# Two-layer graph kernel in fp32: quarter-block weight loads, turns of the scores moved inside the weight stage, half of layer 1's statistics on ScalarE, and another order in the ends

## The chip, the cores and the metric

The kernel runs on one core of one Trainium2 chip. The metric is the device time of that core in microseconds (us), as the median of several executions. One further execution was taken by the hardware profiler; the rows quoted below come from it.

## The reference

The input x has 64 graphs of 256 nodes with 512 features. Both layers normalise, rectify, mix over the graph and add to x. Cut to what matters:

```python
h = relu(layernorm(x))                               # layer 0
q, k, v = h @ Wq.T, h @ Wk.T, h @ Wv.T
rel = adj.T * (q @ k.T)
x = x + (rel / norm(rel, axis=2)) @ v
h = relu(layernorm(x))                               # layer 1
x = x + (adj @ h) @ weight + bias
```

All matrices are fp32. The kernel folds Wq and Wk into one matrix M, so that the scores are g h with g = M h, and it multiplies by two-by-two block schemes of seven products (Strassen and Winograd), some with a second level inside.

## The kernel before

**Tiling.** Two graphs make a pair, so there are 32 pairs (NP = 32); a pair has four chunks of 128 nodes. A ring of five buffers (`x_ring`) holds x for five pairs. The work of several pairs is interleaved: while pair i is in layer 1, pair i+1 is in its scores, pair i+2 in its projections g and v, and pair i+3 is being normalised and transposed.

**Stages.** `before_pairs` forms M from Wq and Wk, looks whether the low bits of adj are zero (this selects between two versions of the loop; with these inputs the exact one runs), transposes adj and Wv, and normalises pair 0. `first_pairs` fills the pipeline, `steady(i)` runs for i = 1 to 28, `last_pairs` drains it. In `steady(i)` the order is: `attend_and_v` (attention of pair i, rest of v), `scores` of pair i+1, `g_and_v` of pair i+2, the gather `py` with adj (`gather_steps`), and the weight stage `mix_and_v` (layer 1's weight product, with the remaining g and v products between).

**What sets the order.** TensorE, VectorE and ScalarE run in exactly the order in which the code emits, written out by hand. A stage is a list of products, and a dictionary `{slot: steps}` says which steps of other engines are emitted behind which product. Each engine works its own list from the front; a step that has to wait holds everything behind it on that engine. A product is followed by its `take`: ScalarE copies the PSUM bank where it is the first into its place, VectorE adds it otherwise.

**Banks.** In `winograd_steps` and `two_levels` most products accumulate into one bank, `bank_a`: product 1, then 6, 7 and 4 on top of it. Each is read by its `take` before the next may be added. The products are called a1, c5, a6, a7, a4; g1 to g4 are the small second-level products in `bank_e` and `bank_d`.

**The names that the change touches.** `norm` (L322) gives the steps of a normalisation: per chunk BN_STATS and BN_AGGREGATE (L333, L334) on VectorE, `root` (L337, L338), `end` (L341, L342) and the ReLUs on ScalarE (L345). `ln1` is layer 1's normalisation; its first four steps are called `halves` in `steady`. `turns` are four VectorE transposes (L592, `turned<-placed`) of the scores, which an earlier step `place` has moved by 16 DMAs (L589) from `rel` to `placed`; `rel_steps` (L176 to L179) form the operands of the attention out of `turned`. `second_of_y` gives `y_second`, eight small VectorE operations for the second level of the weight product. `take` of the weight product is L776, the second level's is L537, that of the scores is L562, that of the attention L672.

In `steady`, `turns` come behind the last product of the gather:

```python
run_steps(y_products, {0: v_steps[1:2], 2: y_steps[0:1], 3: turns})
```

**DMA queues.** At the start SyncE's queue (SP) carries Wq in four row blocks and x of pair 0, ScalarE's queue (ACT) carries adj, then Wk in four row blocks; Wv and the next x follow on ScalarE's queue from inside the M product. Before each pair's transposes 16 small DMAs (L443) move h from one layout to another on SP.

Of the kernel before, what the change touches and what calls it, by code (L numbers as in the profile page):

```python
# [19 lines left out]
def kernel(  # L20
# [61 lines left out]
    X, H, HL, G, V, R, H2, Y, HL2, Y2, second_h = ({} for _ in range(11))  # L82
# [13 lines left out]
    adj_sb = work.tile([P, NC, N], F32, tag="placed", name="adj_sb")  # L96
    w_sb = const.tile([P, DC, D], F32, name="w_sb")
    bias_bc = const.tile([P, D], F32, name="bias_bc")
    nc.scalar.dma_start(out=adj_sb, in_=adj.rearrange("(c p) n -> p c n", p=P))
    for e in range(DC):  # L100
        nc.sync.dma_start(out=wq_sb[:, e], in_=wq[e * P : (e + 1) * P, :])
        nc.scalar.dma_start(out=wk_sb[:, e], in_=wk[e * P : (e + 1) * P, :])
    load(0)
    ones = const.tile([P, 1], F32, name="ones")
    nc.gpsimd.memset(ones, 1.0)
    warm = work.tile([P, P], F32, tag="turned", name="warm")
    nc.gpsimd.memset(warm, 0.0)
    ident = const.tile([P, P], F32, name="ident")
    make_identity(nc, ident)

    def load_wv():
        nc.scalar.dma_start(out=wv_sb, in_=wv.rearrange("(c p) d -> p c d", p=P))

    def load_w_and_bias():
        nc.scalar.dma_start(out=w_sb, in_=weight.rearrange("(c p) d -> p c d", p=P))
# [4 lines left out]
    def flat(t):  # L120
        return t.rearrange("p b c d -> p (b c) d")
# [158 lines left out]
    def run_steps(steps, side):  # L280
        for at, step in enumerate(steps):
            step()
            run(side.get(at, ()))
# [35 lines left out]
        return product  # L319


    def norm(src):  # L322

        st = small.tile([P, TC, 6], F32, tag="st", name="st")
        mv = small.tile([P, TC, 2], F32, tag="mv", name="mv")
        rs = small.tile([P, TC], F32, tag="rs", name="rs")
        nb = small.tile([P, TC], F32, tag="nb", name="nb")  # L330

        def chunk(c):
            nc.vector.bn_stats(st[:, c, :], src[:, c, :])  # L333
            nc.vector.bn_aggr(mv[:, c, :], st[:, c, :])  # L334

        def root():
            nc.vector.tensor_scalar(rs, mv[:, :, 1], 0.0, EPS, op0=ALU.max, op1=ALU.add)  # L337
            nc.scalar.activation(rs, rs, AF.Sqrt)  # L338

        def end():  # L340
            nc.vector.reciprocal(rs, rs)  # L341
            nc.vector.scalar_tensor_tensor(nb, mv[:, :, 0], -1.0, rs, op0=ALU.mult, op1=ALU.mult)  # L342

        def relu(dst, c):
            nc.scalar.activation(  # L345
                dst, src[:, c, :], AF.Relu, bias=nb[:, c : c + 1], scale=rs[:, c : c + 1]
            )

        return [(lambda c=c: chunk(c)) for c in range(TC)], root, end, relu

    def norm_by_scalar(src):

# [37 lines left out]
    def ln0(i):  # L390

        if i == 0:
            H[i] = blocks.rearrange("p c d e -> p c (d e)")
        else:
            H[i] = work.tile([P, TC, D], F32, tag="hy", name=f"h_{i}")
        h = H[i]
        chunks, root, end, relu = norm(flat(X[i]))
        return chunks, root, end, [(lambda c=c: relu(h[:, c, :], c)) for c in range(TC)]

    def relus_of_h(i, relu):  # L400
# [287 lines left out]
        ], side)  # L688


    def ln1(i, exact):


        xt = flat(X[i])
        chunks, root, end, relu = norm(xt)
# [61 lines left out]

    def second_of_y(i, pool_tag="h2"):

        room = work.tile([P, 2, 3, P], F32, tag=pool_tag, name=f"ys2_{i}")  # L760
# [62 lines left out]
    def before_pairs():  # L823
# [16 lines left out]
        stats, root, end, relus = ln0(0)  # L840

        def look():
            nc.vector.tensor_single_scalar(
                low, adj_sb.rearrange("p c n -> p (c n)").bitcast(I32), 0xFFF, op=ALU.bitwise_and
            )
            nc.vector.tensor_reduce(low_max, low, axis=mybir.AxisListType.X, op=ALU.max)
            pf = ps_m.tile([P, 512], F32, tag="pm", name="pf")
# [22 lines left out]
        def take(t, k, bank, first):  # L870
# [4 lines left out]
            else:  # L875
                nc.vector.tensor_add(dst, src, dst)

        look()
        transpose_adj()
        run([right_steps[1], left_steps[1]])  # L880
        winograd(product_weights_moving(m_left, m_factors), take, {
            0: [load_wv, left_steps[2], right_steps[2]],
            1: [left_steps[3], left_steps[0]],
            2: [right_steps[0]] + stats[0:1] + [lambda: load(1, nc.scalar)],
            3: stats[1:4] + [root, lambda: load(2, nc.scalar)],
            4: [end] + relus + [right_steps[3]],
            5: m_steps[0:3] + [transpose_wv],
            6: m_steps[3:4],
        }, early=True)
# [47 lines left out]
    def first_pairs(exact):  # L937
# [50 lines left out]
        if exact:  # L988
            nc.vector.tensor_copy(adjt_r, adjt_sb)
        g, v = g_and_v(2, by_slot(layer_1(parts), {  # L990
            1: h_second + [inverse], 2: turned3[0:4], 3: scales + [place],
            4: add_bias(0) + turned3[4:6], 5: turned3[6:8], 6: sums3[0:1],
        }))
        v_steps, rel_steps = attend_operands(1)
# [6 lines left out]
        run(y_steps[1:2])  # L1001
        mixed = mix_and_v(0, g, v, {
            0: y_steps[2:4] + totals[0:2], 1: y_second[0:4] + totals[2:4],
            2: y_second[4:8] + [mean] + row_squares[0:2], 3: v_steps[1:2] + row_squares[2:4],
            4: turns + rel_steps[0:2] + norm0[0:2], 5: rel_steps[2:4] + v_steps[2:3],
        })
        return norm0[2], v_steps[3:4], mixed, v

    def steady(i, exact, relu0, v_last, mixed, v):
# [3 lines left out]

        gs = g_operands(i + 1)
        relus0 = relus_of_h(i + 3, relu0)
        stats, root, end, relus, uppers, lowers = ln1(i, exact)
        halves = [stats[b * NC + t] for t in range(NC) for b in range(NB)]
        attend_and_v(i, mixed, v, {
            0: relus0[0:2] + v_last, 1: relus0[2:4] + gs[0:1], 2: gs[1:2],
            3: gs[2:3], 4: gs[3:4] + halves[0:1], 5: halves[1:2],  # L1020
        })
        place_blocks(i + 3)
        if i + 4 < NP:
# [1 line left out]
        HL2.pop(i + 1)  # L1025
        h_second = second_h.pop(i + 2)()
        masks, squares, norm_root, inverse, scales, place, turns = scores(i + 1, {
            0: halves[2:3], 1: halves[3:4] + h_second[0:1], 2: [root] + h_second[1:4],
            3: [end] + relus[0:1], 4: relus[1:2],
        }, inside=True)  # L1030
        turned, sums = transpose_blocks(i + 3)
# [7 lines left out]
            5: lowers[3:4] + sums[1:3], 6: sums[3:4] + v_steps[0:1],  # L1039
        })  # L1040
        y_products, y_steps = gather_steps(i, exact)
        run_steps(y_products, {0: v_steps[1:2], 2: y_steps[0:1], 3: turns})
        y_second = second_of_y(i)
        totals, row_squares, mean, root0, end0, relu0 = [], [], [], [], [], None
        if i + 4 < NP:
# [3 lines left out]
        mixed = mix_and_v(i, g, v, {  # L1049
            0: y_steps[2:4] + totals[0:2], 1: y_second[0:4] + totals[2:4],  # L1050
            2: y_second[4:8] + mean + row_squares[0:2],
            3: rel_steps[0:2] + row_squares[2:4], 4: root0 + rel_steps[2:4] + end0,
            5: v_steps[2:3],
        })
        return relu0, v_steps[3:4], mixed, v
# [1 line left out]
    def last_pairs(exact, relu0, v_last, mixed, v):  # L1057
# [59 lines left out]
            m["a1"], m["c5"], m["a6"], m["g1"], lambda: run([m["a7"], m["c"]]), m["g2"], m["a4"],  # L1117
            m["g3"],
        ], {
            0: y_second[0:4] + [root], 1: y_second[4:8] + [end] + relus[0:2] + uppers[0:2],  # L1120
            4: lowers[0:2] + relus[2:4], 5: uppers[2:4] + add_bias(c), 7: lowers[2:4],
        })
        y_products, y_steps = gather_steps(c, exact)
# [44 lines left out]
```

## Time and profile before

| | |
|---|---|
| median of 3 executions | 1706.22 us (1706.12 to 1707.53) |
| the profiled execution's own time | 1703.48 us |
| its span in the profile | 1701.4 us |
| TensorE (PE) busy | 1684.2 us, 99% |
| VectorE (DVE) busy | 1472.9 us, 87% |
| ScalarE (ACT) busy | 811.3 us, 48% |
| GpSimd (POOL) busy | 226.7 us, 13% |
| period of an undisturbed steady pair (gather at 524.85 to gather at 576.57) | 51.72 us |

The profiled execution's own time is 2.1 us above its span (what lies around the span) and 2.7 us below the median. A row of the timeline gives start, duration, engine, source line, operation, output and inputs, and in brackets how long the engine was idle before it and what released it. A matmul's end is modelled, so consecutive rows overlap: eight records of 128x256 are drawn 1.89 us long, but the next group starts 1.73 us later.

### The profile page before, as it was taken

What the parts mean: (1) busy time and instruction counts of PE and PEld (TensorE: products, weight loads), DVE (VectorE), ACT (ScalarE), POOL (GpSimd) and SP (SyncE); (2) the same over time, 40 slices, a digit from 0 to 9 for tenths busy, and PEclk for the clock granted to TensorE, in tenths of its full rate; (3) what the DMA queues carried; (4) which work ended last, traced back from release to release, by engine and by line L of the source; (5) the groups of instructions that cost most, each with busy time, mean ns of one, the idle gap of its engine ahead of it and who ended that gap; (6) DMA issues with size and microseconds to landing.
All of it is one profiled execution on the core that took longest, in us unless ns stands there. A gap on an engine that the chain in (4) does not pass through costs nothing.

```text
span 1701.4 us, 28459 instructions
## 1 busy us (share of the span) xinstructions
PE 1684.2 (99%) x10274; PEld 1530.6 (90%) x10274; DVE 1472.9 (87%) x3312; ACT 811.3 (48%) x1835; POOL 226.7 (13%) x191
## 2 busy tenths in 40 slices
PE   9999999999999999999999999999999999999997
PEld 7979999999899999999999999999999999999986
DVE  7788889888898888898888988888988889888677
ACT  4455444545445554445544455454455544453331
POOL 1211100111101111001111001110011110011111
PEclk9999999999999999999999999999999999999999
DMA  7414332234332233332343322443323433223101
GB/s 247 63 26 87 84 78 57 55 77 87 79 62 68 53 87 85 77 60 63 65 87 80 83 50 50 87 87 77 60 67 60 87 83 80 55 47 62 38 25 53
DMA packets 425734, 122.56 MB, mean 72 GB/s; under 512 B 398064, under 2 KB 398832, under 8 KB 425584
## 3 DMA queue, kind: packets, MB, share of 16 engines
q1 hardware_dynamic: 412992, 80.28, 25.6%
q0 software_dynamic: 8432, 32.51, 5.2%
q10 hardware_dynamic: 4160, 7.87, 1.3%
q8 instruction: 83, 1.36, 0.3%
q14 instruction: 67, 0.55, 0.1%
HBM read 38.27 MB, written 33.55 MB: 42 GB/s over the span
## 4 chain that ended last, share of the span: by engine, by line
PE 91%; DVE 4%; SPq 2%; DMA 1%; ACT 1%; issue 1%; DVEq 0%; ACTq 0%
PE bank_a L302 24%; PE bank_a L290 12%; PE bank_a L314 7%; PE bank_c L302 6%; PE bank_e L528 6%; PE bank_a L665 6%; PE py L742 6%; PE bank_d L528 5%; PE bank_c L314 3%; PE bank_c L290 3%; PE bank_c L665 3%; PE bank_e L481 3%; SPq L589 2%; PE bank_d L481 2%; PE bank_b L314 2%; PE bank_b L665 1%
## 5 line engine op out<-in xcount | busy, mean ns | idle before, releaser
L726 POOL TENSOR_TENSOR x_ring<-x_ring,bias_bc 128x512 f32<-128x512 f32 x128 | 187.2, 1483 | 667.3 <-DVE rel L562 406.2
L302 PE MATMUL bank_a<-wv_t,ht 128*128 128x256 f32 x768 | 181.7, 379 | 0.0
L290 PE MATMUL bank_a<-ht,m_t 128*128 128x256 f32 x768 | 181.4, 379 | 0.0
L290 PEld LDWEIGHTS bank_a<-ht,m_t 128*128 128x128 f32 x768 | 145.9, 190 | 19.8
L302 PEld LDWEIGHTS bank_a<-wv_t,ht 128*128 128x128 f32 x768 | 143.5, 190 | 18.3
L714 DVE TENSOR_TENSOR h<-h2c,h 128x512 fp32r<-128x512 f32 x128 | 85.4, 689 | 80.0 <-ACT h L710 80.0
L516 ACT COPY v<-bank_a 128x512 f32<-128x512 f32 x96 | 55.1, 574 | 206.5 <-PE bank_a L302 206.5
L367 ACT ACTIVATE blocks<-x_ring,sm 128x512 f32<-128x512 f32 x112 | 80.8, 722 | 125.3 <-DVE sm L364 123.5
L742 PE MATMUL py<-adjt_r,h 128*128 128x256 f32 x1024 | 127.1, 281 | 0.5 <-DVE h L714 0.4
L345 ACT ACTIVATE h2c<-x_ring,nb,rs 128x512 f32<-128x512 f32 x128 | 97.3, 809 | 58.0 <-DVE nb L342 51.9
L302 PE MATMUL bank_a<-w_t,ys 128*128 128x256 f32 x512 | 121.4, 380 | 2.2 <-DVE x_ring L776 2.2
L742 PEld LDWEIGHTS py<-adjt_r,h 128*128 128x128 f32 x1024 | 120.9, 189 | 1.0 <-DVE h L714 0.9
L797 POOL DMA_DIRECT2D out_dram<-x_ring x31 | 24.0, 773 | 723.3 <-issue 522.9
L380 ACT ACTIVATE h<-x_ring,nb,rs 128x512 f32<-128x512 f32 x112 | 82.0, 802 | 66.0 <-PE bank_e L528 66.0
L302 PEld LDWEIGHTS bank_a<-w_t,ys 128*128 128x128 f32 x512 | 96.7, 190 | 16.4 <-DVE x_ring L776 3.0
L746 ACT COPY yt<-py 128x512 f32<-128x512 f32 x128 | 74.9, 588 | 70.4 <-PE py L742 47.3
L776 DVE TENSOR_TENSOR x_ring<-bank_a,x_ring 128x512 f32<-128x512 f32 x128 | 87.9, 687 | 23.2 <-PE bank_a L302 23.2
L314 PE MATMUL bank_a<-ht,gt 128*128 128x128 f32 x744 | 101.2, 279 | 0.0
L333 DVE BATCH_NORM_STATS2 st<-x_ring 128x6 f32<-128x512 f32 x144 | 97.6, 678 | 0.4
L560 ACT COPY rel<-bank_a 128x256 f32<-128x256 f32 x96 | 35.7, 372 | 129.6 <-PE bank_a L314 111.1
L314 PEld LDWEIGHTS bank_a<-ht,gt 128*128 128x128 f32 x744 | 90.4, 192 | 2.8
L453 DVE STREAM_TRANSPOSE ht<-blocks 128x256 f32<-128x256 f32 x248 | 87.7, 407 | 0.7 <-DMA blocks<-h 0.7
(223 smaller groups left out, 4012.5 us busy)
## 6 DMA issues: line engine op xcount, KB each, us to landing
blocks<-h SPq DMA_DIRECT2D x496, 64.0 KB, 2.3
out_dram<-x_ring POOLq DMA_DIRECT2D x31, 1024.0 KB, 4.8
x_ring<-in_x_dram SPq DMA_DIRECT2D x28, 1024.0 KB, 5.6
placed<-rel SPq DMA_DIRECT2D x496, 32.0 KB, 2.0
x_ring<-in_x_dram ACTq DMA_DIRECT2D x4, 1024.0 KB, 5.3
wq_sb<-in_L_gnn_Wq_dram SPq DMA_DIRECT2D x4, 256.0 KB, 4.8
wk_sb<-in_L_gnn_Wk_dram ACTq DMA_DIRECT2D x4, 256.0 KB, 6.0
wv_sb<-in_L_gnn_Wv_dram ACTq DMA_DIRECT2D x1, 1024.0 KB, 5.6
```

The costliest lines, as they stand in the source:

```text
L290: nc.tensor.matmul(bank[:, e * HT_ : (e + 1) * HT_], right[n][:, d, ts(e, P)], left[n][:, d, :], start=(start and e == 0 and d == 0), stop ...
L302: nc.tensor.matmul(bank[:, b * HD : (b + 1) * HD], left[n][:, d, ts(b, P)], right[n][:, d, :], start=(start and b == 0 and d == 0), stop=( ...
L314: nc.tensor.matmul(bank[:, ts(b, P)], right[n][:, d, ts(b, P)], left[n][:, d, ts(b, P)], start=(start and b == 0 and d == 0), stop=(d == H ...
L333: nc.vector.bn_stats(st[:, c, :], src[:, c, :])
L345: nc.scalar.activation(dst, src[:, c, :], AF.Relu, bias=nb[:, c : c + 1], scale=rs[:, c : c + 1])
L453: nc.vector.transpose(ht[:, d, half].rearrange("p (b n) -> p b n", b=NB), by_half[:, :, half, d])
L528: nc.tensor.matmul(out, left[k][n], right[k][n], start=start, stop=True, skip_group_check=True)
L665: nc.tensor.matmul(bank[:, ts(b, HD)], left[n][:, b], right[n][:, b], start=(start and b == 0), stop=True, skip_group_check=True,)
L714: nc.vector.tensor_sub(dst[:, 1, c, :], whole_h[c], dst[:, 0, c, :].bitcast(F32))
L726: (lambda c=c: add(xt[:, c, :], xt[:, c, :], bias_bc, ALU.add)) for c in range(TC)
L742: nc.tensor.matmul(pm[:, d, :], left[:, b * NC + m, ts(d0 + d, P)], right, start=(n == 0), stop=(n == len(terms) - 1),)
L776: nc.vector.tensor_add(xt[block], bank.rearrange("p (b e) -> p b e", b=NB), xt[block])
```

## The change

1. Wq and Wk are loaded by quarter blocks (two row chunks by half the columns) in the order in which M's seven products use them; adj comes behind Wk, x of pair 0 behind Wq, and Wv directly behind adj, all before the M product.
2. In `before_pairs` the look at adj, its verdict (`find`) and the transpose of adj move from ahead of the M product to the products numbered 3 and 4 in it; pair 0's statistics become those of item 3.
3. `norm` takes a scratch tile `junk`. With it, chunks 0 and 2 get their sums and their squared deviations from ScalarE (four activations with an accumulator), and two small VectorE operations (`minus`, `variances`) connect them; chunks 1 and 3 stay on VectorE. It is used for pair 0's first normalisation and for layer 1 in `steady`. The scratch lies in the tile of `second_of_y`, made larger.
4. In `steady` the `turns` move from behind the gather into the weight stage, to slot 3, ahead of `rel_steps[0:2]`.
5. In `first_pairs` the scaling and placing of pair 1's scores move from slot 3 to slot 1 of `g_and_v`, ahead of `h_second`, and `turns` from slot 4 to slot 3 of `mix_and_v`.
6. In `last_pairs` the eight operations `y_second` are spread: four behind c5 and four behind a6, in the last two weight stages.

```diff
+    for k in range(2):
+        for j in range(2):
+            block = (slice(None), slice(j * HC, (j + 1) * HC), slice(k * HD, (k + 1) * HD))
+            nc.sync.dma_start(out=wq_sb[block], in_=wq.rearrange("(c p) d -> p c d", p=P)[block])
+            nc.scalar.dma_start(out=wk_sb[block], in_=wk.rearrange("(c p) d -> p c d", p=P)[block])
     nc.scalar.dma_start(out=adj_sb, in_=adj.rearrange("(c p) n -> p c n", p=P))
-    for e in range(DC):
-        nc.sync.dma_start(out=wq_sb[:, e], in_=wq[e * P : (e + 1) * P, :])
-        nc.scalar.dma_start(out=wk_sb[:, e], in_=wk[e * P : (e + 1) * P, :])
     load(0)
+    nc.scalar.dma_start(out=wv_sb, in_=wv.rearrange("(c p) d -> p c d", p=P))
...
+        def totals():
+            for c in (0, 2):
+                nc.scalar.activation(
+                    junk, src[:, c, :], AF.Copy, scale=1.0 / D, accum_out=mv[:, c, 0:1]
+                )
+        def squares():
+            minus = small.tile([P, TC], F32, tag="minus", name="minus")
+            nc.vector.tensor_single_scalar(minus[:, 0::2], mv[:, 0::2, 0], -1.0, op=ALU.mult)
+            for c in (0, 2):
+                nc.scalar.activation(
+                    junk, src[:, c, :], AF.Square, bias=minus[:, c : c + 1],
+                    accum_out=mv[:, c, 1:2],
+                )
+        def variances():
+            nc.vector.tensor_scalar(
+                mv[:, 0::2, 1], mv[:, 0::2, 1], 0.0, 1.0 / D, op0=ALU.max, op1=ALU.mult
+            )
...
+        if junk is not None:
+            chunks = [totals, squares, variances] + chunks[1::2]
...
-        look()
-        transpose_adj()
         run([right_steps[1], left_steps[1]])
         winograd(product_weights_moving(m_left, m_factors), take, {
-            0: [load_wv, left_steps[2], right_steps[2]],
+            0: [left_steps[2], right_steps[2]],
             1: [left_steps[3], left_steps[0]],
-            2: [right_steps[0]] + stats[0:1] + [lambda: load(1, nc.scalar)],
-            3: stats[1:4] + [root, lambda: load(2, nc.scalar)],
-            4: [end] + relus + [right_steps[3]],
+            2: [right_steps[0], lambda: load(1, nc.scalar)],
+            3: stats[0:1] + [look] + stats[1:2] + [right_steps[3], lambda: load(2, nc.scalar)],
+            4: stats[2:] + [root, end] + relus + [find, transpose_adj],
             5: m_steps[0:3] + [transpose_wv],
...
 # first_pairs
-            1: h_second + [inverse], 2: turned3[0:4], 3: scales + [place],
+            1: [inverse] + scales + [place] + h_second, 2: turned3[0:4],
...
-            2: y_second[4:8] + [mean] + row_squares[0:2], 3: v_steps[1:2] + row_squares[2:4],
-            4: turns + rel_steps[0:2] + norm0[0:2], 5: rel_steps[2:4] + v_steps[2:3],
+            2: y_second[4:8] + [mean] + row_squares[0:2],
+            3: turns + v_steps[1:2] + row_squares[2:4], 4: rel_steps[0:2] + norm0[0:2],
+            5: rel_steps[2:4] + v_steps[2:3],
...
 # steady
-            3: gs[2:3], 4: gs[3:4] + halves[0:1], 5: halves[1:2],
+            3: gs[2:3], 4: stats[0:1] + gs[3:4], 5: stats[1:2],
...
-            0: halves[2:3], 1: halves[3:4] + h_second[0:1], 2: [root] + h_second[1:4],
+            0: stats[2:4], 1: stats[4:5] + h_second[0:1], 2: [root] + h_second[1:4],
...
-        run_steps(y_products, {0: v_steps[1:2], 2: y_steps[0:1], 3: turns})
+        run_steps(y_products, {0: v_steps[1:2], 2: y_steps[0:1]})
...
-            3: rel_steps[0:2] + row_squares[2:4], 4: root0 + rel_steps[2:4] + end0,
+            3: turns + rel_steps[0:2] + row_squares[2:4], 4: root0 + rel_steps[2:4] + end0,
...
 # last_pairs
-            0: y_second[0:4] + [root], 1: y_second[4:8] + [end] + relus[0:2] + uppers[0:2],
+            0: [root], 1: y_second[0:4] + [end] + relus[0:2] + uppers[0:2], 2: y_second[4:8],
...
-        ], {0: y_steps[2:4], 1: y_second})
+        ], {0: y_steps[2:4], 1: y_second[0:4], 2: y_second[4:8]})
```

More of the change, by code (lines that the diff above doesn't have):

```diff
@@ L80 @@
     ps_m = ctx.enter_context(tc.tile_pool(name="ps_m", bufs=8, space=bass.MemoryType.PSUM))
-    X, H, HL, G, V, R, H2, Y, HL2, Y2, second_h = ({} for _ in range(11))
+    X, H, HL, G, V, R, H2, Y, HL2, Y2, second_h, junk = ({} for _ in range(12))
     ring = [const.tile([P, NB, NC, D], F32, name=f"x_ring{n}") for n in range(5)]
@@ L109 @@
     make_identity(nc, ident)
-    def load_wv():
-        nc.scalar.dma_start(out=wv_sb, in_=wv.rearrange("(c p) d -> p c d", p=P))
     def load_w_and_bias():
@@ L319, in product_of_tokens, with norm @@
         return product
-    def norm(src):
+    def norm(src, junk=None):
         st = small.tile([P, TC, 6], F32, tag="st", name="st")
@@ L347, in relu @@
             )
-        return [(lambda c=c: chunk(c)) for c in range(TC)], root, end, relu
+        chunks = [(lambda c=c: chunk(c)) for c in range(TC)]
+        if junk is not None:
+            chunks = [totals, squares, variances] + chunks[1::2]
+        return chunks, root, end, relu
     def norm_by_scalar(src):
@@ L396, in ln0 @@
         h = H[i]
-        chunks, root, end, relu = norm(flat(X[i]))
+        chunks, root, end, relu = norm(flat(X[i]), None if i else h[:, 0, :])
         return chunks, root, end, [(lambda c=c: relu(h[:, c, :], c)) for c in range(TC)]
@@ L688, in attend_and_v, with ln1 @@
         ], side)
-    def ln1(i, exact):
+    def ln1(i, exact, junk=None):
         xt = flat(X[i])
-        chunks, root, end, relu = norm(xt)
+        chunks, root, end, relu = norm(xt, junk)
         H2[i] = work.tile([P, 2, TC, D], F32R if exact else F32, tag="h2", name=f"h2_{i}")
@@ L758, in second_of_y @@
     def second_of_y(i, pool_tag="h2"):
-        room = work.tile([P, 2, 3, P], F32, tag=pool_tag, name=f"ys2_{i}")
+        rooms = 6 if pool_tag == "hs2" else 10
+        room = work.tile([P, rooms * P], F32, tag=pool_tag, name=f"ys2_{i}")
+        junk[i] = room[:, 6 * P :]
+        room = room[:, : 6 * P].rearrange("p (k r n) -> p k r n", k=2, n=P)
         factors, steps = {}, []
@@ L846, in look, with find @@
             nc.vector.tensor_reduce(low_max, low, axis=mybir.AxisListType.X, op=ALU.max)
+        def find():
             pf = ps_m.tile([P, 512], F32, tag="pm", name="pf")
@@ L1015, in steady @@
         relus0 = relus_of_h(i + 3, relu0)
-        stats, root, end, relus, uppers, lowers = ln1(i, exact)
-        halves = [stats[b * NC + t] for t in range(NC) for b in range(NB)]
+        stats, root, end, relus, uppers, lowers = ln1(i, exact, junk.pop(i - 1))
         attend_and_v(i, mixed, v, {
             0: relus0[0:2] + v_last, 1: relus0[2:4] + gs[0:1], 2: gs[1:2],
-            3: gs[2:3], 4: gs[3:4] + halves[0:1], 5: halves[1:2],
+            3: gs[2:3], 4: stats[0:1] + gs[3:4], 5: stats[1:2],
         })
```

## The prediction

> **What bounds the kernel now.** I read the page's busy table first, then the waits of TensorE, then the timeline of one steady pair, of pair 0 and of both ends.
>
> ```profile
> PE 1684.2 (99%) x10274; PEld 1530.6 (90%) x10274; DVE 1472.9 (87%) x3312; ACT 811.3 (48%) x1835; POOL 226.7 (13%) x191
> ```
>
> The waits of TensorE (us in total, times, longest):
>
> ```profile
> PE bank_c L302 <- DVE yt L177: 2.3, 5, 0.6
> PE bank_a L302 <- DVE x_ring L776: 2.2, 3, 1.1
> PE bank_e L528 <- DVE x_ring L537: 1.8, 2, 1.6
> ```
>
> TensorE is the bound: 17 us idle in 1701. A wait given to TensorE is added to the span; work taken from VectorE or ScalarE helps only where TensorE waits. The five waits on L177 are those where `turns` sat waiting for their DMAs, the 1.6 is in pair 0, those on L776 in the last weight stages. So the change aims at real idle time, but a small one. The question is what its moves put in the way.
>
> The weight stage of one steady pair (start us, duration us):
>
> ```profile
> 588.42 0.41 DVE L537 TENSOR_TENSOR x_ring<-bank_d,x_ring 128x256 f32<-128x256 f32 x1
> 588.75 0.41 DVE L176 TENSOR_TENSOR rel<-turned 128x256 f32<-128x256 f32 x1
> ...
> 589.20 0.43 DVE L177 TENSOR_TENSOR turned<-turned 128x256 f32<-128x256 f32 x1
> ...
> 589.96 0.69 DVE L776 TENSOR_TENSOR x_ring<-bank_a,x_ring 128x512 f32<-128x512 f32 x1 [0.33 <-PE bank_a L302]
> ...
> 590.65 0.61 PE L481 MATMUL bank_e<-ht,m_t 128*128 128x128 f32 x4
> 591.09 1.89 PE L302 MATMUL bank_a<-w_t,yt 128*128 128x256 f32 x8
> ```
>
> L776 takes product a7 out of `bank_a`; a4 (591.09) is added to that bank next. VectorE waits 0.33 us for a7, ends the take at 590.65, and a4 starts 0.44 later. That is all the cover here: from 582.05 to 589.63 VectorE ran without a gap.
>
> Pair 0 already has its `turns` in the weight stage, a slot later:
>
> ```profile
> 123.30 1.41 DVE L592 STREAM_TRANSPOSE turned<-placed 128x256 f32<-128x256 f32 x4
> ...
> 126.87 0.41 DVE L537 TENSOR_TENSOR x_ring<-bank_e,x_ring 128x256 f32<-128x256 f32 x1
> ...
> 127.43 0.46 PE L528 MATMUL bank_e<-w_t,yt 128*128 128x128 f32 x2 [1.63 <-DVE x_ring L537]
> ```
>
> There TensorE loses 1.63 us: the take behind the transposes is late. This is the change's placing, seen in the kernel before.
>
> [...] rows keep the order of the code, and groups drawn 1.89 us long follow each other after 1.73; I use starts. [...] Wk's last block, issued at 4.7 beside x of pair 0, came into use at 10.6.
>
> **The change part by part.**
>
> *Turns in the weight stage (28 steady pairs).* Removed: four transposes behind the gather, where VectorE had cover; its take of a1 waited 0.32 us for TensorE after them. There c5 started 0.10 late (1.83 after a1 against 1.73). That comes back in every pair, and in the five pairs whose DMAs were late another 0.45: -2.2 us together. Added at 588.75, ahead of L176: the transposes, whose start-to-start is 1.34 (579.75 to 581.09). With everything 0.08 earlier, they run from 588.67; L176 depends on the last one and follows at 590.1, L177 at 590.55, the take of a7 at 590.95, done at 591.65 with its 0.05 of signal. TensorE, 0.10 earlier, was ready for a4 at 590.99: it waits about 0.67, **+0.57 a pair** against before. What follows keeps its distance: VectorE stays 0.4 behind a4 as before (take 593.38, bank ready 593.02), so nothing is won back. By the bounds: 0.45 if the dependent steps cost nothing extra, 0.70 if they cost 0.1 each. Queued behind the transposes are the takes of a7, g2 and g4, the root of the next normalisation (ScalarE) and its DMAs on SP; all slip with TensorE, none is waited for.
>
> *Half the statistics of layer 1 (28 pairs).* Removed from VectorE: two BN_STATS and BN_AGGREGATE, 0.8 each; added: two operations of 0.17. That relief lies in the attention and scores stages, where in these rows TensorE waits for VectorE once:
>
> ```profile
> 611.41 1.06 PE L314 MATMUL bank_b<-ht,g 128*128 128x128 f32 x8
> ...
> 611.90 0.42 DVE L562 TENSOR_TENSOR rel<-bank_a,rel 128x256 f32<-128x256 f32 x1
> ...
> 612.37 1.16 PE L314 MATMUL bank_a<-ht,gt 128*128 128x128 f32 x8
> ```
>
> The last product follows the take of `rel` by 0.05. VectorE had run to it without a gap from 608.04, the third BN_STATS: 3.86 us. After: ScalarE copies v at 603.92 to 604.50, totals two chunks at 0.82 each (L361's rows) to 606.14; `minus` at 606.32 (behind L537, as the first statistics were); two squares at 0.84 (L367's rows) from 606.52 to 608.18; `variances` at 608.2; the remaining chunks' BN_STATS only at 608.3. From there the same 3.86 to the take: 612.15, **+0.25 a pair**. Bounds: 0 (accumulator reads overlap) to 0.40. ScalarE's first copy of `rel` slips from 608.03 to 608.2 and ends at 608.57, before the 608.73 at which a6 needs the bank: no cost, with 0.15 us of cover.
>
> *Start.* The first matmul of M stood at 6.47, the next waited for Wk until 7.99, then to 10.58; from 11.98 to 26.0 TensorE had no gap. With quarter blocks and adj behind them the first products run from 4.9 (end of the warm-up). In the trace packets of 1,024 bytes took 46 ns and those of 2,048 bytes 84, so the 2.1 MB in short rows take 128 x 46 ns = 5.9 us on each of 16 DMA engines: all landed near 8.5, c5 at 9.2 against 11.98. With pf and the transposes of adj (0.6) inside, TensorE is through M about 2.1 us earlier. But what then releases it is pair 0's normalisation:
>
> ```profile
> 19.07 2.93 ACT L345 ACTIVATE blocks<-x_ring,nb,rs 128x512 f32<-128x512 f32 x4 [0.68 <-DVE nb L342]
> ...
> 22.36 1.91 PE L431 MATMUL pt<-ident,blocks 128*128 128x128 f32 x16
> ...
> 23.32 2.05 ACT L434 COPY ht<-pt 128x512 f32<-128x512 f32 x4
> ```
>
> x of pair 0 landed at 12.1; now it comes behind all of Wq and shares with adj and Wv: 8.2 + 2.1 MB at 0.385 MB per us = 13.7 (totals can't start before the copy of a6, 13.4, anyway). Then totals 1.64, `minus` 0.25, squares 1.69, `variances` 0.1, two chunks 1.5, to the ReLU 0.85: first ReLU at 19.8; ReLUs 2.83, then on ScalarE adj's copy 0.5 (before at 6.67), Wv's 0.94, M's 0.48: the first `ht` copy at 24.55, against 23.32. **+1.2**, from -1.5 (if the chain is as short as before) to +2.5. SP's and GpSimd's reading of the branch value slips from 6.3 to 20; their next work stood at 36 and 23.5. ScalarE's table load waits behind Wv's issue, to 7.4; its first copy is needed at 10.9.
>
> *Pair 0.* Earlier `turns` run about 119.8 to 121.1; the take of a7 then delays a4 by 0.3 and g4 by 0.3 instead of 1.63, and smaller gaps behind it (0.34 together) mostly stay: -1.2. But the scales (1.71, L582) now stand on ScalarE ahead of the copy of g's a6 (99.06): it slips to 100.7, and a7 (100.36) waits until 101.35: +1.0. **-0.2**, from -1.5 to +1.
>
> *Ends.* In the last two weight stages four small operations (1.06) leave the way to the take of a6: the waits of 0.78 and 1.14 before a7 shrink, by 0.94 (with the `end` before it) and 1.05. The other four, now behind a6, end 0.8 us before g2 needs them. **-2.0**, from -2.5 to -1.
>
> *Sum:* 28 x 0.82 = 23.0, -2.2, +1.2, -0.2, -2.0: **+19.8 us** on the profiled execution (span 1701.4, own time 1703.5, so 1723.3). The median is 2.7 above that execution; on it, 1726.0.
>
> **Rivals.** *The transposes fit (faster).* If VectorE's lateness at L776 stays inside 0.33 idle + 0.44 of cover, so if they cost it under 0.77 instead of 1.34, a4 isn't held, c5 keeps its 0.10 in 28 pairs (-2.8), and without the scores' wait: -2.8 - 2.2 + 1.2 - 0.2 - 2.0 = -6.0, 1700 us. For it: five late pairs exist, and VectorE does less in all. Against it: L592's own rows, and pair 0's 1.63. *Nothing to tell.* The added wait is some 0.2 a pair and eats the gains: within 3 us of 1706. Needs both terms at a third. *ScalarE late as well (slower still).* If the squares end 0.15 us later than worked out, a6 of the scores waits too; 0.3 a pair gives +8 more, 1734. For it: it is a chain of six handovers, each estimated at 0.03 to 0.05. That the moves aren't made is excluded by the order of the instructions: the four transposes stand between L537 and L176 in every steady pair.
>
> **How the numbers follow.** Slower by the forecast's mechanism, ScalarE's included: 0.83; the transposes fit: 0.13; nothing to tell: 0.04. A measurement of this kernel can tell about 0.2%, 3.4 us, from no change. The likeliest gives 1726. The lows of the two steady terms, 28 x 0.45, and the other terms at their lows give 1711; the highs, 28 x 1.1 less 2.2 with the start at +2.5, give 1735. Range 1713 to 1736, leaving out the faster case.
>
> **What would show it.** In the changed profile: a steady period near 52.5 instead of 51.72; in TensorE's waits `bank_a` on x_ring's take (L804 there) some 0.6 us in 28 pairs, and no waits on `yt`; the last scores product later by 0.25 behind its take; the first `ht` copy after 24; no wait above 0.3 before a7 in the last two stages. It would be wrong if the steady period is at or below 51.7, or if a4 follows g4 without a gap.

## The result, and the profile after

The changed kernel takes 1731.51 us (median of 4 executions, 1731.14 to 1732.0), the kernel before 1706.88 us beside it: ratio 1.0144, 95% interval 1.0126 to 1.0162, so slower by 24.6 us. The forecast was 1726.0 in a range of 1713 to 1736, and slower with 0.83. The profiled execution of the changed kernel took 1732.0 us, its span is 1730.1 at a granted clock of 0.999. The span of before was 1701.4, so the two traces differ by 28.7, about 4 more than the medians: the profiled execution of before lay 3.4 below the median it has here, that of after 0.5 above.

The busy table and the chain that ended last, of the changed kernel:

```profile
PE 1692.6 (98%) x10274; PEld 1533.0 (89%) x10274; DVE 1430.8 (83%) x3254; ACT 895.2 (52%) x2067; POOL 220.3 (13%) x191
...
PE 60%; DVE 25%; SPq 5%; ACT 4%; issue 3%; DMA 2%; DVEq 0%; ACTq 0%
```

VectorE has 42 us less to do than before and ScalarE 84 more, yet the chain now runs through VectorE for 25% of the span (4% before, where TensorE had 91%). Less busy is not earlier. The waits of TensorE (us in total, times, longest):

```profile
PE bank_a L302 <- DVE x_ring L804: 18.5, 29, 0.7
PE bank_a L314 <- DVE rel L587: 2.2, 13, 0.3
PE bank_e L553 <- DVE x_ring L562: 1.6, 2, 1.4
```

L804 is the take of the weight product (L776 before): 3 waits have become 29, one for each of 28 steady pairs and one in the ends. The waits on `yt`, where the transposes behind the gather had waited for their DMAs, are gone.

One steady weight stage of the changed kernel (start us, duration us, idle before it in brackets):

```profile
598.82 1.41 DVE L617 STREAM_TRANSPOSE turned<-placed 128x256 f32<-128x256 f32 x4
600.27 0.43 DVE L176 TENSOR_TENSOR rel<-turned 128x256 f32<-128x256 f32 x1
600.54 0.61 PE L506 MATMUL bank_e<-ht,m_t 128*128 128x128 f32 x4
...
601.07 0.68 DVE L804 TENSOR_TENSOR x_ring<-bank_a,x_ring 128x512 f32<-128x512 f32 x1
601.81 1.99 PE L302 MATMUL bank_a<-w_t,yt 128*128 128x256 f32 x8 [0.66 <-DVE x_ring L804]
```

The four transposes, L176, L177 and the take follow each other without a gap, and a4 (601.81) starts 0.06 behind the end of the take. It follows the small product before it (600.54, g4 in the prediction) by 1.27 us, against 0.44 before: it is 0.83 late, of which the row draws 0.66 as idle, because consecutive rows overlap by 0.17. And the scores of the same pair:

```profile
619.02 0.17 DVE L354 TENSOR_SCALAR mv<-mv 128x2 f32<-128x2 f32 x1 [0.49 <-ACT ys L348]
...
622.22 1.06 PE L314 MATMUL bank_b<-ht,g 128*128 128x128 f32 x8
622.96 0.41 DVE L587 TENSOR_TENSOR rel<-bank_a,rel 128x256 f32<-128x256 f32 x1
623.43 1.16 PE L314 MATMUL bank_a<-ht,gt 128*128 128x128 f32 x8
```

VectorE stands 0.49 us for ScalarE's squares (L348) in front of `variances`, and everything behind it is late: the last scores product follows `bank_b`'s group by 1.21 instead of 0.96.

Where the 28.7 us lie, from the starts of the gathers `py` (pair number as in the code):

| stretch | before | after | difference | forecast |
|---|---|---|---|---|
| start to gather of pair 0 | 107.24 | 110.60 | +3.36 | +1.2 (start), +1.0 (scales) |
| to gather of pair 1 | 54.06 | 53.22 | -0.84 | -1.2 |
| 27 steady periods | 27 x 51.836 | 27 x 52.787 | +25.70 | +20.8, with the next row |
| one more period | 51.72 | 52.39 | +0.67 | |
| from gather of pair 29 to the end | 88.82 | 88.63 | -0.19 | -2.0 |
| sum | 1701.4 | 1730.1 | +28.7 | +19.8 |

The first steady pair's scores lie in the second row, ahead of the gather of pair 1. With the statistics alone (stats_only, below) that row is 54.32, so 0.26 of it is their wait, and the earlier `turns` of pair 0 gave 1.10.

### The profile page after: what moved, and what is told of

It is laid out like the page before. It is cut to its first block, busy times and chain, and to the rows that moved or that the text cites. A ratio compares the mean times of both kernels' runs of the same rounds, so it can differ in the third digit from the quotient of the medians.

```text
span 1730.1 us, 28627 instructions
## 1 busy us (share of the span) xinstructions
PE 1692.6 (98%) x10274; PEld 1533.0 (89%) x10274; DVE 1430.8 (83%) x3254; ACT 895.2 (52%) x2067; POOL 220.3 (13%) x191
## 3 DMA queue, kind: packets, MB, share of 16 engines
q8 instruction: 83, 1.36, 0.3%
## 4 chain that ended last, share of the span: by engine, by line
PE 60%; DVE 25%; SPq 5%; ACT 4%; issue 3%; DMA 2%; DVEq 0%; ACTq 0%
PE bank_a L302 15%; PE bank_a L290 13%; PE py L767 7%; DVE x_ring L804 6%; SPq L468 5%; PE bank_c L302 4%; PE bank_a L690 3%; PE bank_c L290 3%; PE bank_a L314 3%; PE bank_e L553 3%; DVE turned L617 2%; PE bank_e L506 2%; PE bank_d L506 2%; DVE st L335 2%; DVE ys L178 2%
## 5 line engine op out<-in xcount | busy, mean ns | idle before, releaser
L751 POOL TENSOR_TENSOR x_ring<-x_ring,bias_bc 128x512 f32<-128x512 f32 x128 | 180.7, 1432 | 686.2 <-ACT h2c L367 656.0
L697 DVE TENSOR_TENSOR x_ring<-bank_a,x_ring 128x512 f32<-128x512 f32 x116 | 79.5, 685 | 39.6 <-PE bank_a L690 39.6
L804 DVE TENSOR_TENSOR x_ring<-bank_a,x_ring 128x512 f32<-128x512 f32 x128 | 87.6, 685 | 17.6 <-PE bank_a L302 17.5
L492 ACT COPY g<-bank_a 128x512 f32<-128x512 f32 x96 | 56.0, 583 | 56.6 <-PE bank_a L290 56.6
```

What stands on the lines that cost most here:

```text
L751: (lambda c=c: add(xt[:, c, :], xt[:, c, :], bias_bc, ALU.add)) for c in range(TC)
L804: nc.vector.tensor_add(xt[block], bank.rearrange("p (b e) -> p b e", b=NB), xt[block])
```

## The experiments

### How many transposes fit into the weight stage

Theory: the loss comes only from VectorE being late at the take of a7, and there is a limit below which this costs nothing. Rival: ScalarE's statistics carry the loss, or each transpose costs in proportion. Three kernels from the changed one, with none, two and three of the four steady transposes left in the weight stage, and the kernel before with the statistics alone.

```diff
 # turns_back
-        run_steps(y_products, {0: v_steps[1:2], 2: y_steps[0:1]})
+        run_steps(y_products, {0: v_steps[1:2], 2: y_steps[0:1], 3: turns})
...
-            3: turns + rel_steps[0:2] + row_squares[2:4],
+            3: rel_steps[0:2] + row_squares[2:4],
 # turns_two: 3: turns[0:2] behind the gather, turns[2:4] in the weight stage
 # turns_three: 3: turns[0:1] behind the gather, turns[1:4] in the weight stage
 # stats_only: the kernel before with the junk tile, and in steady
-        stats, root, end, relus, uppers, lowers = ln1(i, exact)
+        stats, root, end, relus, uppers, lowers = ln1(i, exact, junk.pop(i - 1))
...
```

Expected of none inside:

> The changed kernel with the four steady transposes back behind the gather, all else kept. Theory (in the weight stage they make VectorE late for the take of a7, and TensorE waits there in each of 28 pairs): a4 follows g4 by 0.44 again, the wait of bank_a on the weight product's take is gone from TensorE's list, the steady period falls from 52.7-52.8 to near 52.0 (the scores' 0.25 stays), and the time is some 16 us below the changed kernel: about 1716 (1712 to 1720). Rival (ScalarE's statistics carry most of the loss): it stays within 4 us of the changed kernel, 1728 to 1732.

Of two inside:

> The changed kernel with two of the four steady transposes behind the gather and two in the weight stage. Theory (there are 0.33 us of idle VectorE and 0.44 of distance between the end of the take and a4, so 0.77 us of cover; two transposes with a start-to-start of 0.335 each are 0.67): no wait before a4, time like that with all four behind the gather, 1714 to 1719. Rival (no cover: what stands ahead of the take costs TensorE in proportion): half of the 0.83 us stays, 28 x 0.41 = 11.6 us above that, some 1727.

Of three inside:

> The changed kernel with one steady transpose behind the gather and three in the weight stage. Theory of a threshold: 3 x 0.335 = 1.00 less 0.77 of cover leaves a drawn wait of 0.24 before a4 (and about 0.1 that a waited group costs beyond it): 28 x 0.24 to 0.34 = 7 to 9.5 us above the kernel with two there, 1722 to 1727. Proportional rival: three quarters of 0.83, 17 us above all four behind the gather, about 1732.

Of the statistics alone:

> The kernel before with layer 1's statistics of two chunks on ScalarE in the 28 steady pairs, and nothing else. Theory (the two chunks left on VectorE stand behind an operation that waits for ScalarE's squares, and the take ahead of the last scores product ends 0.25 later): last scores product 1.21 behind bank_b's group instead of 0.96, +7 us, 1714 (1711 to 1717). Rival 1 (VectorE is relieved of 1.3 us a pair, so its takes come earlier): 1703 to 1706. Rival 2 (these statistics are the main loss): +18 to +24.

Measured (before beside them: 1705.96 us; the undisturbed period is the median of the 27 steady ones):

| transposes in the weight stage | time, us | ratio to before (95%) | undisturbed period, us |
|---|---|---|---|
| 0 | 1714.32 | 1.0045 (1.0029 to 1.0062) | 51.98 |
| 2 | 1713.58 | 1.0044 (1.0027 to 1.0060) | 52.07 |
| 3 | 1722.04 | 1.0092 (1.0075 to 1.0109) | 52.40 |
| 4 (the change) | 1731.51 | 1.0144 (1.0126 to 1.0162) | 52.83 |
| statistics alone, transposes as before | 1713.88 | 1.0042 (1.0025 to 1.0059) | 51.98 |

The first two transposes together cost 0.09 us, the third 0.33 and the fourth 0.43: a limit, not a proportion. With three inside, the list of TensorE's waits has the row

```profile
PE bank_a L302 <- DVE x_ring L804: 9.0, 28, 0.3
```

which is 0.32 a pair (0.24 was expected); with two inside only the one of the ends is left in it. TensorE in the weight stage with two inside:

```profile
594.80 0.61 PE L506 MATMUL bank_e<-ht,m_t 128*128 128x128 f32 x4
...
595.41 1.99 PE L302 MATMUL bank_a<-w_t,yt 128*128 128x256 f32 x8
```

Here a4 follows g4 by 0.61 where 0.44 is the undisturbed distance, though no wait is drawn: two are already 0.17 beyond the limit. What c5 and a6 win, 0.17 together, pays for that. The 0.09 of the table is left because the next product follows a4 by 1.83 instead of 1.73. Two transposes take 0.67, so the room is about 0.50, not the 0.77 assumed; at 0.33 a transpose, one fits.

The loss of the weight stage is thus some 16 us of the 25 (24.6 for four inside less 8.4 for none, each against the kernel before beside it). The statistics alone give +0.25 a period, from 51.73, and +7.9 us: they are the rest of it. Their trace has the wait that was worked out for them (the last scores product 1.21 behind `bank_b`'s group), and the relief of VectorE by 1.3 us a pair gave nothing back.

### The statistics with VectorE's own chunks first

If what costs the 0.25 is VectorE standing for the squares, it should take its own two chunks first.

```diff
 # stats_own_first: from stats_only
-            chunks = [totals, squares, variances] + chunks[1::2]
+            chunks = [totals, squares] + chunks[1::2] + [variances]
```

> As stats_only, but VectorE takes the statistics of its own two chunks first and only then the operation that waits for ScalarE's squares. Theory (what delays the last scores product is VectorE standing for ScalarE): chunk 1 starts at 0.05 behind the last take of the attention instead of 0.9, the take of rel comes 0.5 earlier and no longer holds the product; undisturbed period 51.64 instead of 51.98 (before: 51.73), time 1703 to 1706. Rival (ScalarE's accumulating operations hold the bank copies of the scores): 51.9 to 52.0 and 1713 to 1715 as in stats_only.

Measured: 1712.17 us, ratio 1.0035 (1.0023 to 1.0048), undisturbed period 51.92. The forecast of the time failed, but not on its first step:

```profile
613.25 1.06 PE L314 MATMUL bank_b<-ht,g 128*128 128x128 f32 x8
614.14 1.06 PE L314 MATMUL bank_a<-ht,gt 128*128 128x128 f32 x8
```

The last scores product follows `bank_b`'s group by 0.89, so the wait is gone, and 0.32 is won there, with 0.10 more behind it. The period and the time are those of the rival, but its mechanism is not in the trace: no scores product waits for a copy. The gain is given back a stage later (rows of all engines, in order of time):

```profile
614.43 2.94 POOL L749 TENSOR_TENSOR x_ring<-x_ring,bias_bc 128x512 f32<-128x512 f32 x2 [14.75 <-ACT h2c L365]
614.69 3.24 DVE L588 TENSOR_TENSOR rel<-rel,adjt_sb 128x512 f32<-128x512 f32 x2
...
622.47 0.58 ACT L490 COPY g<-bank_a 128x512 f32<-128x512 f32 x1
...
623.10 1.99 PE L290 MATMUL bank_a<-ht,m_t 128*128 128x256 f32 x8
```

The ReLUs of layer 1 come earlier, and behind them GpSimd's addition of the bias (L749) now starts just ahead of the two masks (L588), which take 3.24 us from start to end instead of 2.36 (612.84 to 615.20). In the kernel before the first mask came 0.08 ahead of the addition and took 0.68; only the second was long:

```profile
613.97 1.23 DVE L565 TENSOR_TENSOR rel<-rel,adjt_sb 128x512 f32<-128x512 f32 x1 [0.45 <-ACT rel L560]
```

It ends 0.55 behind the end of the addition (612.92 to 614.66). L588 reads `rel` and `adjt_sb`, both in SBUF. Here both masks come behind an addition and take 1.56 and 1.76, and each ends 0.55 behind one. By what means an addition on GpSimd holds a mask on VectorE is not shown. The scaling on ScalarE, which needs both masks, then holds back g's copies (L490, at 622.47 above), and a7 of g starts 1.99 behind the product before it instead of 1.73: 0.26, and 0.10 more in its own group. Against the kernel before, 0.17 is won at the scores and 0.37 lost here, which is the 0.20 of the period. That this is the whole path from the masks to g was read from the trace and not tried by itself.

### The start

```diff
 # start_only: the kernel before with the loads and before_pairs of the change
 # start_vector: from it, pair 0's statistics without junk
-            3: stats[0:1] + [look] + stats[1:2] + [right_steps[3], lambda: load(2, nc.scalar)],
-            4: stats[2:] + [root, end] + relus + [find, transpose_adj],
+            3: stats + [root, end] + relus + [look, right_steps[3], lambda: load(2, nc.scalar)],
+            4: [find, transpose_adj],
```

> The kernel before with the changed start alone (order of the loads, look and transposes of adj inside the M product, pair 0's statistics half on ScalarE). Theory (TensorE's earlier M product is given back because pair 0's normalisation runs through ScalarE and stands behind the copy of a6, and because the product c5 waits for Wk's last block and two additions): the first product of g stands 1 to 2.5 us later than in the kernel before (24.11), the time 1708 to 1709. Rival (the start gains what the M product gains): first product of g near 22, time 1704 to 1705.

> The same start, with pair 0's four chunks of statistics on VectorE as soon as x is there, root, end and ReLUs issued directly behind them, and the look at adj and the last operand of M behind those. Theory (it is the first ReLU that releases TensorE's transposes, and then the last products of M): first ReLU near 18.0 instead of 20.9; the take of M's sixth product slips to 21.0, so the last product starts at 21.1 as before, and the first product of g stands near 25: between the kernel before and the changed start, 1706.5 to 1708. Rival (it is the loads' landing that holds the start, not this chain): the first product of g stays at 26 and the time at 1708 to 1709.

Measured: start_only 1706.78 us against 1705.49, ratio 1.0008 (0.9999 to 1.0016), a hair slower and not to be told from no change by time. The trace tells more, because this stretch can be compared in every profile: the first product of g starts at 25.97 to 26.26 in the five kernels with the changed start, and at 23.79 to 25.81, on average 24.43, in the eight with the old loads. So the changed start costs 1.6 us on average, and in these profiles it scatters less. Of the changed kernel:

```profile
8.92 0.69 DVE L135 TENSOR_TENSOR wk_t<-wk_sb 128x512 f32<-128x512 f32 x1 [8.92 <-DMA wk_sb<-in_L_gnn_Wk_dram]
9.76 0.69 DVE L177 TENSOR_TENSOR m_room<-wq_sb 128x512 f32<-128x512 f32 x1
...
10.51 1.99 PE L302 MATMUL bank_c<-wk_t,m_room 128*128 128x256 f32 x8 [1.40 <-DVE m_room L177]
...
20.88 2.93 ACT L367 ACTIVATE blocks<-x_ring,nb,rs 128x512 f32<-128x512 f32 x4 [0.51 <-DVE low_any L879]
...
26.26 2.05 PE L290 MATMUL bank_a<-ht,m_sb 128*128 128x256 f32 x8 [0.76 <-ACT ht L459]
```

The chain is the one foreseen, but c5 (10.51) is 1.3 us later than forecast: VectorE needs two additions behind the last block of Wk (8.92), one after the other. ScalarE's totals (14.75) stand directly behind the copy of a6, as foreseen, and at the first `ht` copy (25.61, forecast 24.55) 1.06 of the 1.3 is left.

start_vector missed: 1709.51 us, ratio 1.0025 (1.0017 to 1.0033), and the first product of g at 29.68. The first ReLU did come at 18.55, near the 18.0 expected, but the look at adj now stood behind the statistics, and the small product `pf` that reads its result stands on TensorE ahead of M's sixth product:

```profile
19.62 0.19 PE L850 MATMUL pf<-ones,low_max 128*1 128x1 f32 x2 [3.92 <-DVE low_max L846]
```

The look had been moved without asking which instruction of another engine waits for it. More than the wait was lost: from 19.6 to 24.1 us the granted clock is 0.50 in this profile (1.00 in the changed kernel in the same stretch), and M's sixth product takes 3.41 us to the next start, where it took 1.73 before. So this kernel does not tell the loads from the chain apart, and how much of the 1.6 us each holds stays open.

### The ends

```diff
 # ends_only: the kernel before with the change in last_pairs
-            0: y_second[0:4] + [root], 1: y_second[4:8] + [end] + relus[0:2] + uppers[0:2],
+            0: [root], 1: y_second[0:4] + [end] + relus[0:2] + uppers[0:2], 2: y_second[4:8],
...
-        ], {0: y_steps[2:4], 1: y_second})
+        ], {0: y_steps[2:4], 1: y_second[0:4], 2: y_second[4:8]})
 # ends_late_relus: in the first of the two stages instead
+            0: [root], 1: y_second[0:4], 2: y_second[4:8] + [end] + relus[0:2] + uppers[0:2],
 # ends_no_bias: as ends_only, without add_bias(c): the last pair's output lacks the bias
-            4: lowers[0:2] + relus[2:4], 5: uppers[2:4] + add_bias(c), 7: lowers[2:4],
+            4: lowers[0:2] + relus[2:4], 5: uppers[2:4], 7: lowers[2:4],
```

The question came from the trace of the changed kernel (the stage before the last, all engines):

```profile
1698.95 2.68 POOL L751 TENSOR_TENSOR x_ring<-x_ring,bias_bc 128x512 f32<-128x512 f32 x2 [14.75 <-DVE ys L178]
1699.14 1.36 DVE L178 TENSOR_TENSOR ys<-ys 128x128 f32<-128x128 f32 x1
...
1700.54 1.24 DVE L179 TENSOR_TENSOR ys<-ys,ys 128x128 f32<-128x128 f32 x1
...
1702.17 0.71 PE L553 MATMUL bank_e<-w_t,ys 128*128 128x128 f32 x4 [1.42 <-DVE x_ring L562]
```

Two of the four small operations that moved behind a6 are drawn 1.36 and 1.24 us long instead of 0.28: each ends 0.15 behind one of GpSimd's two bias additions (2.68 for both). The take in front of g2 is late by 1.4. Like the masks, these operations read two inputs from SBUF. Is it GpSimd, or the order?

> The kernel before with the changed order of the eight small operations in the last two weight stages alone. Theory (in the last stage the wait of 1.14 before a7 goes; in the stage before it the wait of 0.78 goes but comes back before g2, because the last two small operations, which read two operands from SBUF, run beside GpSimd's bias addition and take 1.3 us each instead of 0.28): 1.42 before g2 as in the changed kernel, and in all 0 to -0.5, 1706.2 to 1706.9. Rival (the forecast's sum, the slow ones being chance): 1704.5 to 1705.

> As ends_only, but in the stage before the last the end of the normalisation and the first two ReLUs, after which GpSimd adds the bias, come behind the second four of the small operations. Theory (the small operations meet no bias addition): 0.28 us for each of the eight, a wait before g2 of at most 0.2 instead of 1.42, time from the last but one gather to the end 1 to 2 us below the kernel before, 1704.5 to 1706. Rival (the wait before g2 has to do with the order on VectorE alone): about 1 us stays before g2 and the time is like that of ends_only.

> As ends_only, without the addition of the bias to the last pair (so the output of that pair lacks it): GpSimd has nothing to do in the stage before the last. Theory (two-operand VectorE operations on SBUF are held up while GpSimd adds the bias): the last two small operations take 0.28 us instead of 1.37 and 1.24, the wait of 1.42 before g2 goes, and the two subtractions of the lower parts take 0.64 each; the stretch from the last but two gather (L742, some 1615) to the end is 86.5 to 87.2 instead of 88.34. Rival (order on VectorE): the 1.42 and the 88.34 stay.

| kernel | time, us | ratio to before (95%) | gather of pair 29 to the end |
|---|---|---|---|
| before | 1705.49 | | 88.82 |
| ends_only | 1704.96 | 0.9994 (0.9985 to 1.0002) | 88.34 |
| ends_late_relus | 1705.20 | 0.9994 (0.9986 to 1.0002) | 87.54 |
| ends_no_bias (before beside it: 1706.58) | 1703.92 | 0.9984 (0.9977 to 0.9991) | 86.20 |

In ends_only the 1.24 and the wait of 1.42 before g2 are there again, as expected. Without the bias addition the two small operations are back at 0.28, and the wait before g2 is gone:

```profile
1673.75 0.28 DVE L178 TENSOR_TENSOR ys<-ys 128x128 f32<-128x128 f32 x1
...
1675.19 0.61 PE L528 MATMUL bank_e<-w_t,ys 128*128 128x128 f32 x4
```

That settles it: GpSimd, not the order. With late ReLUs, the small operations are free as well, but the additions run from 1674.75 and meet the next two-input operation instead:

```profile
1675.91 2.37 DVE L714 TENSOR_TENSOR h<-h2c,h 128x512 fp32r<-128x512 f32 x2
```

(1.28 for the same two before), and TensorE waits 1.45 before g3. A later wait of 0.4 in the last gather goes, so in all 1.3 us is won, inside what was expected in the trace though the times alone can't show it.

### What the parts give together

The first try to put together what had won something:

```diff
 # together: stats_own_first with two transposes inside, pair 0's turns a slot earlier, ends_late_relus
+        run_steps(y_products, {0: v_steps[1:2], 2: y_steps[0:1], 3: turns[0:2]})
+            3: turns[2:4] + rel_steps[0:2] + row_squares[2:4],
 # one_inside: the kernel before (statistics on VectorE, start as it was), with the ends of ends_late_relus and
+        run_steps(y_products, {0: v_steps[1:2], 2: y_steps[0:1], 3: turns[0:3]})
+            3: turns[3:4] + rel_steps[0:2] + row_squares[2:4],
 # and, as in the first, in first_pairs
+            3: turns + v_steps[1:2] + row_squares[2:4], 4: rel_steps[0:2] + norm0[0:2],
```

> The kernel before with stats_own_first, two steady transposes in the weight stage and two behind the gather, pair 0's transposes a slot earlier (its scaling left where it was), and the ends of ends_late_relus; the start as before. Theory, in sums of what the other runs showed: steady pairs 51.64 + 0.09 and nearly no late pairs against 51.84 on average, 27 x -0.1 = -3; pair 0's step to pair 1 53.2 instead of 54.06; ends -1.3: about -5, 1699.5 to 1702.5. Rival (with VectorE freer, the weight stage's cover shrinks or the late transfers wait elsewhere): 1704 to 1707.

> The kernel before with three steady transposes behind the gather and one in the weight stage (its lateness, 0.335 us, is inside the cover of 0.67), pair 0's transposes a slot earlier with its scaling left where it was, and the ends of ends_late_relus. Theory: undisturbed period 51.73 as before; pair 0's step to pair 1 53.2 instead of 54.06; from the third last gather to the end 87.5 instead of 88.8; pairs held by late transfers only partly fewer: 2 to 4 us below the kernel before, 1702 to 1704.5. Rival (the bias addition of GpSimd or another step held by VectorE takes it back): no difference from the kernel before, 1705.5 to 1707.

Measured: together 1708.52 us against 1706.58, ratio 1.0013 (1.0007 to 1.0020), a miss: its expectation was made before the 51.92 of stats_own_first was known (51.64 had been assumed), and its period is 0.10 above 51.92, 52.02. Its other terms came: pair 0 to pair 1 in 53.06, the end in 87.69, and no period above 52.3.

one_inside takes 1697.98 us against 1706.56, ratio **0.9952 (0.9938 to 0.9966)**: 8.6 us faster than the kernel before, more than twice what was expected. Its weight stage:

```profile
586.46 0.44 DVE L592 STREAM_TRANSPOSE turned<-placed 128x256 f32<-128x256 f32 x1
...
587.73 0.68 DVE L776 TENSOR_TENSOR x_ring<-bank_a,x_ring 128x512 f32<-128x512 f32 x1
...
588.18 0.61 PE L481 MATMUL bank_e<-ht,m_t 128*128 128x128 f32 x4
588.63 1.89 PE L302 MATMUL bank_a<-w_t,yt 128*128 128x256 f32 x8
```

The take has lost its 0.33 of idle time and a4 still follows the product before it (588.18) by 0.45. The undisturbed period is 51.57, below the 51.73 of before: a1, c5 and a6 follow each other by 1.73 without the 0.10 and 0.07 that each lost before, and this time the gain is not paid back at a4. By stretches, of 6.6 us between the spans (1694.8 and 1701.4): 27 steady periods of 51.69 on average, -3.9; pair 0's step, 52.89, -1.2; the end, 87.52, -1.3; the start, where nothing was changed, -0.2. The rest of the 8.6 is that the profiled executions lay differently to their medians, 3.1 and 1.2 below.

## Why the prediction was right, and where its sum was off

**The bound and the sign: right.** TensorE had no slack, one added wait of VectorE per pair set the time, and the named place was the right one (L804 before a4).

**Turns, +0.57 forecast, +0.74 or +0.86 measured.** The drawn wait of 0.66 meets the forecast 0.67 by chance: what was worked out there is the whole delay of a4, and that is 0.83. The step that failed is "With everything 0.08 earlier". The transposes start 8.70 us behind a1 (590.12 to 598.82), exactly as L176 did before (580.05 to 588.75): VectorE's list hangs on the end of a1, not on c5, so what TensorE won at c5 and a6 (0.17) only made it wait longer. From a1 to a4 it is 11.04 before and 11.69 after, +0.65. Then a group that had to wait is followed 0.10 later than one that had not (1.83 against 1.73), a cost that I left out. Together they go beyond the upper bound of 0.70, narrowly. And in 15 of 29 pairs the gather took 3.85 instead of 3.73. In the kernel before 12 did as well, but the undisturbed period there is 51.72 to 51.73 with either, as a6 starts no later for it; here it is 52.71 with one and 52.83 with the other. The sum did not have this either.

**The late transfers, -2.2: right in kind.** The average period of before stood 0.11 above the undisturbed one, 2.9 us over 27; none of it is left after.

**Scores, +0.25: right**, by the change itself (1.21 against 0.96) and by stats_only (51.98 against 51.73). The rival of a further late ScalarE fell: no scores product before the last waits.

**Start, +1.2: right chain, size in doubt.** 2.15 in the one profile, 1.6 on average over the profiles. The step that failed is "all landed near 8.5, c5 at 9.2": the last block was in use at 8.92, and two additions follow it, not one.

**Pair 0, -0.2: measured about +0.1.** The scales ahead of g's copy cost a wait of 0.77 (1.0 forecast); with what lies behind it the gather of pair 0 came 1.2 later than the start explains (3.36 less 2.15), and the turns gave 1.1 of the 1.2 expected, once the first scores' wait is taken out of that row. The scales were not run by themselves; the turns gave 1.2 in one_inside as well.

**Ends, -2.0: wrong, -0.2.** The last stage gave its 1.05 (a1 to a7 takes 6.32 instead of 7.37). In the other, "end 0.8 us before g2 needs them" failed: the four small operations were priced from rows where GpSimd stood still. The trace of before showed what the sum left out: in 29 pairs the second mask takes 1.23 us beside the bias addition, where the first takes 0.68, and in pair 0 an L179 takes 1.38 where others take 0.43.

The terms of the turns (by 5.8), the ends (1.8), the start (0.9) and pair 0 (0.3) were all too low, so the sum missed 8.9 of 28.7 us between the traces. The median differs from the forecast by only 5.5, and that is no merit of the sum: the profiled execution of before was a short one.

## What to carry to other kernels

Find what each engine's list hangs on before crediting a gain: a wait removed on TensorE is won only if the engine that must release it later hangs on the same event (here 0.17 us was won at c5 and a6, and none of it at a4). A place for a moved step has a measurable room (here about 0.5 us, which is one transpose of four): move as much as fits and leave the rest, as one_inside does, instead of all or nothing. And when an operation moves, look at what GpSimd does beside its new place (here two operations of 0.28 us became 1.36 and 1.24).

## What the hardware showed that I had not expected

A VectorE operation held up by GpSimd was not drawn as idle: it showed as a longer operation (1.36 instead of 0.28), so VectorE's list of waits did not name it; only the row's own duration did. Operations with one input in PSUM (the takes) were not lengthened beside the same additions: in the kernel before, 30 takes of g out of `bank_c` (L469) lie wholly beside one and take 0.65 to 0.69, against 0.69 for the one that no GpSimd operation overlaps. A wait of 3.9 us on TensorE went together with a granted clock of 0.50, and the next product took twice as long (start_vector). And with the changed start, loads and order together, the first product of g came at the same time within 0.3 us in five kernels, against 2.0 in eight, though later; which of its parts does that was not tried.
